# Two tiles per statistics operation, and a VectorE bias in place of a table product, in a graph-network layer on one core

## The chip, the cores and the metric

The kernel runs on one core of a Trainium2 chip. The core has five engines with a queue of instructions each: TensorE (PE in the profile; its weight loads are PEld), VectorE (DVE), ScalarE (ACT), GpSimd (POOL) and SyncE (SP), which here issues DMAs. [...] Matrix products go to PSUM[...]; everything else lies in SBUF. The metric is the time of one execution on the device in microseconds (us), lower is better.

## The reference

128 graphs of 64 nodes with 128 features each. Every pair of nodes gets a message from a three-layer perceptron, the messages are masked by the adjacency matrix and summed, and a second perceptron updates the nodes. Between the layers stand layer normalisations.

```python
def _mlp(x, w0, b0, g0, be0, w1, b1, g1, be1, w2, b2):
    h = relu(x @ w0 + b0)
    h = _layernorm(h, g0, be0)
    h = relu(h @ w1 + b1)
    h = _layernorm(h, g1, be1)
    return h @ w2 + b2

pair_feats = concatenate([f_i, f_j], axis=-1)
messages = _mlp(pair_feats, msg_w0, ..., msg_b2)
messages = messages * coupling_matrix[..., None]
agg = sum(messages, axis=2)
upd_in = concatenate([part_feats, agg], axis=-1)
updated = part_feats + _mlp(upd_in, upd_w0, ..., upd_b2)
```

Only the variance of each normalisation is needed row by row: the mean is taken out by centring the next layer's weights (`w1c`). The scale by 1/std is put off as well. If layer 0's standard deviation is sd, relu((h/sd) @ w1c + b1) is relu(h @ w1c + sd * b1)/sd. So layer 1's bias is a product of a row (b1) and a column (sd of each edge).

## The kernel before, in words

The graph is sparse, so the kernel lists the existing edges only. Two graphs make a pair, a pair has room for 2 x 640 edges, which are ten tiles of 128 edges. Four tiles make a chunk (`CH = 4`), and there are 160 chunks (`NCHK`). Five chunks make a group q of twenty tiles (`QT = 20`, `QC = 5`), of which there are 32 (`NQ`). Four pairs, ten chunks, make a block (`CPB = 10`), which ends in an update of its nodes; a `Unit` is such an update.

A chunk goes through these stages:

- `layer0` (L550): products of PE into the one bank `hps`; ACT takes the relu out of it into `h`, features on the partitions (L559).
- `stats0` (L561): PE transposes the four tiles of `h` into the one bank `hT` (L565), and DVE takes the statistics of each tile by one `bn_stats` (L569). Such an operation gives six numbers per edge: count, mean and squared deviations of the elements at even places, and the same for the odd ones.
- `layer1` (L616): PE adds h @ w1c onto a bank z that already holds sd * b1 (L626), and ACT takes the relu out into `y` (L629). There are two z banks, taken in turn.
- `stats1` (L631): four more `bn_stats`, on `y` in SBUF (L636).
- later the weights (L702, POOL) and the sums over the edges (`reduce`, L717).

After five chunks of `stats0`, `var0_of` (L575) has POOL join the two halves of each statistic into a sum of squares (`square_sum`, L247: five operations of 20 columns), and `root_of` (L578) has ACT take the root, sd. `var1_step` (L638) does the same for layer 1 with the term eps * variance of layer 0. For the last group DVE does it in POOL's place.

The bias sd * b1 comes into a z bank in two ways. In most chunks (those of `seed`, L605, called at L933: digits 0, 1, 2, 5, 6, 7, 9 of n mod 10, from chunk 2 to 151, the first block without 5) ACT writes b1 times the column sd, one tile at a time (L614). In the others, among them the last eight chunks, PE writes it by one product before its own (L623). For this product, `bias_rows` to `bias_part` (L641 to L679) build a table `b1t` of 80 rows at the start, which has b1 in two parts of shorter numbers, and for each group `root_of` splits sd in two parts (L583 on ACT, L584 on POOL), `turn_root` (L587) turns them by PE, and `root_out` (L592) has ACT copy the result to `sdT`.

The order of all work is written out by hand. `at(n, place, fn)` puts a call into step n of a plan, and the loop at the end walks the steps. Within a step the order is: places a, m and s, `layer1` of chunk n - L1 (L1 = 8), place b, `layer0` of chunk n, `stats0` of chunk n - 1, place k, `stats1` of chunk n - L1, places x, x1, x2, e0, e1, e. Each engine takes its share of these calls in just this order. A seed for chunk n stands at place x of step n + 6, so behind `stats1` of chunk n - 2, which used the same z bank. The update units use `square_sum` and `bn_stats` in the same way (`layer_out`, L781; `upd_m0`; `upd_m1`).

Of the kernel before, what the change touches and what calls it, by code (L numbers as in the profile page):

```python
# [9 lines left out]
F32 = mybir.dt.float32  # L10
# [8 lines left out]
EPS = 1e-5  # L19
# [5 lines left out]
def tile_gnn(  # L25
# [221 lines left out]
    def square_sum(stp, st, n, name, eng=nc.gpsimd, m20=None):  # L247

        d = stp.tile([P, n], F32, name=name + "_d")
        s = stp.tile([P, n], F32, name=name + "_s")  # L250
        m2 = stp.tile([P, n], F32, name=name)
        eng.tensor_tensor(d, st[:, :, 1], st[:, :, 4], op=ALU.subtract)  # L252
        eng.tensor_tensor(s, st[:, :, 2], st[:, :, 5], op=ALU.add)
        if eng is nc.vector:
            if m20 is not None:
                eng.scalar_tensor_tensor(s, m20, EPS, s, op0=ALU.mult, op1=ALU.add)
            eng.scalar_tensor_tensor(d, d, C / 4.0, d, op0=ALU.mult, op1=ALU.mult)
        else:
            eng.tensor_tensor(d, d, d, op=ALU.mult)
            eng.tensor_scalar(d, d, C / 4.0, None, op0=ALU.mult)  # L260
        eng.tensor_tensor(m2, d, s, op=ALU.add)
        return m2

# [6 lines left out]
    def var1_of(stp, st, m20, n, name, eng=nc.gpsimd):  # L270

        if eng is nc.vector:
            return square_sum(stp, st, n, name, eng, m20)
        v = stp.tile([P, n], F32, name=name + "_v")
        eng.tensor_scalar(v, m20, EPS, None, op0=ALU.mult)
        m2 = square_sum(stp, st, n, name, eng)
        eng.tensor_tensor(v, v, m2, op=ALU.add)
        return v
# [16 lines left out]
    def rstd1_of(stp, st, m20, n, name):  # L295
        return inverse(stp, root1(stp, var1_of(stp, st, m20, n, name), n, name), n, name)


    def edge_path(es):
# [45 lines left out]
        TP, S, H, ST0, V0, SD, SH, Y, ST1, Q, OH, WT, YS, MK, D, IR, JR, SR, Z = ({} for _ in range(19))  # L345
# [215 lines left out]
        def stats0(n):  # L561
            q, c = divmod(n, QC)
            ps = ps_t.tile([P, CH, P], F32, name="hT")
            for t in range(CH):
                nc.tensor.transpose(ps[:, t, :], H[n][:, t * P:(t + 1) * P], ident)  # L565
            if c == 0:
                ST0[q] = stp.tile([P, QT, 6], F32, name="st0", bufs=2)
            for t in range(CH):
                nc.vector.bn_stats(ST0[q][:, CH * c + t, :], ps[:, t, :])  # L569

        def eng_of(q):

            return nc.vector if q == NQ - 1 else nc.gpsimd

        def var0_of(q):  # L575
            V0[q] = square_sum(stp, ST0.pop(q), QT, "m20", eng_of(q))

        def root_of(q):  # L578

            sd = SR[q] = root0(stp, V0[q], QT, "m20")  # L580
            SH[q] = lp.tile([P, 4, QT], F32R, name="sh", bufs=2)
            sdb = sd.unsqueeze(1).to_broadcast([P, 2, QT])
            nc.scalar.copy(SH[q][:, 0:2, :], sdb)  # L583
            nc.gpsimd.tensor_tensor(SH[q][:, 2:4, :], sdb, SH[q][:, 0:2, :].bitcast(F32),  # L584
                                    op=ALU.subtract)

        def turn_root(q):  # L587
            SD[q] = abank()
            nc.tensor.transpose(SD[q][0:4 * QT, 0:P],
                                SH.pop(q).rearrange("p j t -> p (j t)").bitcast(F32), ident)  # L590

        def root_out(q):  # L592
            t = lp.tile([4 * QT, P], F32R, name="sdT")
            nc.scalar.copy(t, SD[q][0:4 * QT, 0:P])
            SD[q] = t

        SEEDED = set()
# [6 lines left out]

        def seed(n):  # L605

            q, c = divmod(n, QC)
            z_of(n)  # L610
            SEEDED.add(n)
            for t in range(CH):
                k = CH * c + t
                nc.scalar.activation(Z[n][:, t, :], W["b1b"], AF.Copy, scale=SR[q][:, k:k + 1])  # L614

        def layer1(n):  # L616

            q, c = divmod(n, QC)
            ps = z_of(n)
            del Z[n]  # L620
            h = H.pop(n)
            if n not in SEEDED:
                nc.tensor.matmul(ps, lhsT=SD[q], rhs=W["b1t"][:, CH * c:CH * c + CH, :],  # L623
                                 start=True, stop=False, skip_group_check=True)
            for t in range(CH):
                nc.tensor.matmul(ps[:, t, :], lhsT=h[:, t * P:(t + 1) * P], rhs=W["w1c"],  # L626
                                 start=False, stop=True, skip_group_check=True)
            Y[n] = yp.tile([P, CH, C], F32, name="y")
            nc.scalar.activation(Y[n], ps, AF.Relu)  # L629

        def stats1(n):  # L631
            q, c = divmod(n, QC)
            if c == 0:
                ST1[q] = stp.tile([P, QT, 6], F32, name="st1", bufs=2)
            for t in range(CH):
                nc.vector.bn_stats(ST1[q][:, CH * c + t, :], Y[n][:, t, :])  # L636

        def var1_step(q):  # L638
            Q[q] = var1_of(stp, ST1.pop(q), V0.pop(q), QT, "m21", eng_of(q))

        def bias_rows():  # L641

            own = const.tile([P, 4, QT], F32, name="own")
            nc.gpsimd.memset(own, 0.0)
            nc.gpsimd.affine_select(out=own, in_=own, pattern=[[-QT, 4], [-1, QT]],
                                    compare_op=ALU.not_equal, fill=1.0, base=0,
                                    channel_multiplier=1)

            sel = const.tile([P, 2, QT], F32, name="sel")
            nc.gpsimd.tensor_tensor(sel, own[:, 0:2, :], own[:, 2:4, :], op=ALU.add)  # L650
            W["tile_of"] = const.tile([P, QT], F32, name="tile_of")
            nc.gpsimd.tensor_tensor(W["tile_of"], sel[:, 0, :], sel[:, 1, :], op=ALU.add)
            W["sel"] = sel

        def bias_parts():
            W["part"] = const.tile([P, 2], F32, name="part")
            nc.vector.tensor_reduce(W["part"], W.pop("sel"), axis=AX.X, op=ALU.add)

        def bias_table():

            K = 4 * QT
            part, tile_of = W.pop("part"), W["tile_of"]
            hi = const.tile([P, C], F32R, name="b1hi")
            nc.scalar.copy(hi, W["b1b"])
            lo = const.tile([P, C], F32, name="b1lo")
            nc.gpsimd.tensor_tensor(lo, W["b1b"], hi.bitcast(F32), op=ALU.subtract)
            nc.gpsimd.tensor_scalar(lo, lo, part[:, 1:2], None, op0=ALU.mult)
            mix = const.tile([P, C], F32, name="b1mix")
            nc.gpsimd.tensor_scalar(mix, hi.bitcast(F32), part[:, 0:1], None, op0=ALU.mult)
            nc.gpsimd.tensor_tensor(mix, mix, lo, op=ALU.add)  # L670
            W["b1t"] = const.tile([K, QT, C], F32R, name="b1t")
            W["b1mix"], W["tile_of"] = mix[0:K], tile_of[0:K]

        def bias_part(c):
            t = slice(CH * c, CH * c + CH)
            nc.gpsimd.tensor_tensor(W["b1t"][:, t, :],
                                    W["b1mix"].unsqueeze(1).to_broadcast([4 * QT, CH, C]),
                                    W["tile_of"][:, t].unsqueeze(2).to_broadcast([4 * QT, CH, C]),
                                    op=ALU.mult)  # L679
# [101 lines left out]
        def layer_out(u, o, bias):  # L781
            t = wide(o, u)
            add_relu(t, u.l_ps, getattr(u, bias))
            setattr(u, o, t)
            st = updp.tile([P, PB, 6], F32, name=o + "_st", bufs=2)[:, 0:u.n, :]
            for q in range(u.n):
                nc.vector.bn_stats(st[:, q, :], t[:, q, :])
            u.st = st

        def upd_m0(u):  # L790
            u.m2 = square_sum(updp, u.st, u.n, "um0" + u.tag, u.eng)
# [14 lines left out]
        def upd_m1(u):  # L806
            u.v1 = var1_of(updp, u.st, u.m2, u.n, "um1" + u.tag, u.eng)
# [111 lines left out]
        for q in range(NQ):  # L919
# [5 lines left out]
            at(*((n + 1, "x1") if last else (n + 1 if q else QC + 1, "x")), turn_root, q)  # L925
            at(n + 2 if q else QC + 2, "a", root_out, q)
# [6 lines left out]
        for n in range(2, NCHK - L1):  # L933
            if n % CPB in (0, 1, 2, 6, 7, 9) or (n > CPB and n % CPB == 5):
                at(n + L1 - 2, "x", seed, n)


# [25 lines left out]
        bias_rows()  # L963
# [35 lines left out]
        bias_parts()  # L999
# [33 lines left out]
        at(3, "e", bias_table)  # L1033
        for n, k in ((2, 2), (3, 3), (4, 2), (5, 2)):
            at(n, "e", keep_busy, k)
        for c in range(QC):
            at(4 + c, "e", bias_part, c)

# [235 lines left out]
```

## Time and profile before

| | us |
|---|---|
| median of three runs | 549.38 (547.74 to 549.64) |
| the profiled execution | 547.41 |
| its span, first to last instruction | 545.6 |
| PE, DVE, ACT, POOL busy in 200 to 300 us | 100.0, 93.3, 94.3, 67.1 |
| the same in 500 to 520 us | 18.3, 16.3, 11.4, 8.1 |
| the same in 520 to 546 us | 16.4, 14.8, 9.2, 9.1 |
| seeds by ACT, L614 (416 of 128x128) | 154.7 busy, 372 ns each |
| table products, L623 (56 of 80x512) | 26.9 busy, 480 ns each |
| turning of the root, L589 (32) | 9.2 busy, 289 ns each |
| copies for it on ACT, L583 and L594 (32 each) | 7.2 and 8.2 busy |
| small arithmetic of the statistics on POOL, L252 (62 of 128x20) | 15.9 busy, 257 ns each |
| L490, DVE product of 128x512 from PSUM (30) | 20.4 busy, 681 ns each |

Busy time is the time in which an engine works on at least one instruction. An instruction's own duration is longer than the share of time that it takes from its engine, since neighbours overlap: what a queue loses to an instruction is read from the distance between starts in the timeline. The granted clock of PE is 0.995 of full speed over the span.

### The profile page before, as it was taken

What the parts mean: (1) busy time and instruction counts of PE and PEld (TensorE: products, weight loads), DVE (VectorE), ACT (ScalarE), POOL (GpSimd) and SP (SyncE); (2) the same over time, 40 slices, a digit from 0 to 9 for tenths busy, and PEclk for the clock granted to TensorE, in tenths of its full rate; (3) what the DMA queues carried; (4) which work ended last, traced back from release to release, by engine and by line L of the source; (5) the groups of instructions that cost most, each with busy time, mean ns of one, the idle gap of its engine ahead of it and who ended that gap; (6) DMA issues with size and microseconds to landing.
All of it is one profiled execution on the core that took longest, in us unless ns stands there. A gap on an engine that the chain in (4) does not pass through costs nothing. (4 is left out here: it accounts for less than half of the span.)

```text
span 545.6 us, 16370 instructions
## 1 busy us (share of the span) xinstructions
PE 526.1 (96%) x5599; PEld 483.6 (89%) x5599; DVE 479.5 (88%) x1941; ACT 479.6 (88%) x1153; POOL 328.8 (60%) x934
## 2 busy tenths in 40 slices
PE   8999899999999999999999999999999999998984
PEld 7787789999999999999999999999999999988873
DVE  6778789898989899898989989898999989897765
ACT  6788989898999999999999989999999999996534
POOL 3445466665657676665667666566766666556342
PEclk9999999999999999999999999999999999999998
DMA  4484655545684545547555564558456544651401
GB/s 101 103 163 112 145 98 139 119 117 123 120 158 109 143 117 129 127 101 167 119 134 102 140 128 112 145 122 142 113 140 128 123 112 113 142 96 25 46 22 44
DMA packets 90772, 63.26 MB, mean 116 GB/s; under 512 B 57398, under 2 KB 74812, under 8 KB 90684
## 3 DMA queue, kind: packets, MB, share of 16 engines
q1 hardware_dynamic: 90396, 62.03, 52.8%
q8 instruction: 46, 0.75, 0.6%
q14 instruction: 42, 0.34, 0.2%
q10 hardware_dynamic: 288, 0.13, 0.1%
HBM read 6.82 MB, written 4.19 MB: 20 GB/s over the span
## 5 line engine op out<-in xcount | busy, mean ns | idle before, releaser
L626 PE MATMUL z<-w1c,h 128*128 128x128 f32 x1280 | 172.0, 277 | 0.0
L626 PEld LDWEIGHTS z<-w1c,h 128*128 128x128 f32 x1280 | 160.7, 192 | 7.7 <-issue 2.8
L614 ACT ACTIVATE z<-b1b,m_sd 128x128 f32<-128x128 f32 x416 | 154.7, 372 | 10.1
L569 DVE BATCH_NORM_STATS2 st<-hT 128x6 f32<-128x128 f32 x640 | 139.7, 279 | 21.4 <-PE hT L565 21.3
L636 DVE BATCH_NORM_STATS2 st<-y 128x6 f32<-128x128 f32 x640 | 137.5, 276 | 1.9 <-ACT y L629 1.4
L629 ACT ACTIVATE y<-z 128x512 f32<-128x512 f32 x160 | 94.9, 593 | 20.3 <-PE z L626 19.6
L559 ACT ACTIVATE h<-hps,b0c 128x512 f32<-128x512 f32 x160 | 109.8, 686 | 1.1 <-PE hps L556 1.0
L565 PE MATMUL hT<-ident,h 128*128 128x128 f32 x640 | 97.7, 275 | 2.1 <-DVE st L569 1.6
L556 PE MATMUL hps<-s,abl 128*128 128x512 f32 (+3 forms) x256 | 91.8, 370 | 0.9 <-ACT h L559 0.4
L565 PEld LDWEIGHTS hT<-ident,h 128*128 128x128 f32 x640 | 74.5, 141 | 15.8 <-DVE st L569 7.1
L556 PE MATMUL hps<-s,abh 128*128 128x512 f32 (+3 forms) x256 | 77.9, 323 | 0.0
L702 POOL TENSOR_TENSOR w<-oh,m_q 128x192 f32<-128x192 f16 x126 | 64.7, 526 | 4.5 <-PE ys L717 3.3
L252 POOL TENSOR_TENSOR m_d<-st 128x20 f32<-128x20 f32 x62 | 15.9, 257 | 76.0 <-DVE st L569 62.2
L538 DVE TENSOR_TENSOR j<-mk,cmpt 128x320 fp32r<-128x320 f32 x124 | 58.6, 473 | 1.0 <-PE mk L530 1.0
L514 POOL CAST i<-tp 128x640 fp32r<-128x640 f16 x58 | 41.6, 718 | 27.9 <-issue 15.1
L499 ACT ACTIVATE d<-slot,mid 128x640 f16<-128x640 f16 x64 | 53.2, 831 | 0.2 <-DVE mid L423 0.2
L556 PEld LDWEIGHTS hps<-s,abl 128*128 128x128 f32 x256 | 48.9, 191 | 1.8 <-ACT h L559 0.9
L556 PEld LDWEIGHTS hps<-s,abh 128*128 128x128 f32 x256 | 48.9, 191 | 0.0
L717 PE MATMUL ys<-y,w 128*32 128x128 f32 x1488 | 47.0, 275 | 0.0
L717 PEld LDWEIGHTS ys<-y,w 128*32 128x32 f32 x1488 | 38.7, 110 | 4.1 <-issue 3.6
L490 DVE TENSOR_TENSOR abl<-mu,abh 128x512 fp32r<-128x512 f32 (+1 forms) x32 | 21.3, 664 | 19.6 <-ACT abh L484 19.6
L530 PE MATMUL mk<-tp,posall 128*128 128x320 f16 x126 | 37.7, 299 | 0.4 <-DVE tp L505 0.4
(243 smaller groups left out, 991.1 us busy)
## 6 DMA issues: line engine op xcount, KB each, us to landing
s<-i SPq DMA_DIRECT2D x124, 160.0 KB, 2.7
s<-j SPq DMA_DIRECT2D x124, 160.0 KB, 2.7
xn<-in_x_dram SPq DMA_DIRECT2D x15, 256.0 KB, 3.9
out_dram<-uo SPq DMA_DIRECT2D x15, 256.0 KB, 2.4
an<-in_adj_dram SPq DMA_DIRECT2D x16, 128.0 KB, 2.8
oh<-tp SPq DMA_TRANSPOSE x64, 3.5
xn<-in_x_dram SPq DMA_DIRECT2D x2, 128.0 KB
out_dram<-uo SPq DMA_DIRECT2D x2, 128.0 KB, 2.6
```

The source lines that it names most:

```text
L499: nc.scalar.activation(D[p], slot, AF.Abs, bias=blocks[b]["mid"][:, q:q + 1], scale=-1.0)
L538: nc.vector.tensor_tensor(JR[p][:, c], MK.pop((p, k))[:, 0:HC], cmpt[:, c], op=ALU.is_equal)
L556: nc.tensor.matmul(ps[:, c:c + w], lhsT=ab[:, g % 4, :], rhs=s, start=(k == 0), stop=(k == 1))
L559: nc.scalar.activation(H[n], ps, AF.Relu, bias=b0c)
L565: nc.tensor.transpose(ps[:, t, :], H[n][:, t * P:(t + 1) * P], ident)
L569: nc.vector.bn_stats(ST0[q][:, CH * c + t, :], ps[:, t, :])
L614: nc.scalar.activation(Z[n][:, t, :], W["b1b"], AF.Copy, scale=SR[q][:, k:k + 1])
L626: nc.tensor.matmul(ps[:, t, :], lhsT=h[:, t * P:(t + 1) * P], rhs=W["w1c"], start=False, stop=True, skip_group_check=True)
L629: nc.scalar.activation(Y[n], ps, AF.Relu)
L636: nc.vector.bn_stats(ST1[q][:, CH * c + t, :], Y[n][:, t, :])
L702: (nc.vector if p == NP - 2 else nc.gpsimd).tensor_tensor(WT[p][:, g], oh, qs, op=ALU.mult)
L717: nc.tensor.matmul(YS[b][g * N + m * HN:g * N + (m + 1) * HN, k, :], lhsT=w[:, g, m, u, :], rhs=y, start=(u == 0), stop=(u == TH - 1), til ...
```

## The change

Statistics: two tiles are taken by one `bn_stats`. Its stream takes an element of the first tile, then one of the second, and so on, so that the elements at even places are the first tile and those at odd places the second. The two sums of squared deviations that come out are those of the two tiles, and nothing has to be joined: `var0_of` becomes a view, and layer 1's variance is the view plus the term of layer 0, two operations on POOL in place of seven. This holds for the edge tiles (hT in PSUM, y in SBUF) and for the update.

Bias: the table, its building and the turning of the root are gone. Chunks with the digits 3, 4 and 8 (in the first block 1 and 5 too) and the odd ones of the last eight get their bias from DVE, by one product of 128x512 into the z bank; ACT seeds those that it did, and chunk 0 and the even ones of the last eight. Two products `prime` the z banks at the start.

```diff
+    def two_stats(st, src):
+
+        nc.vector.bn_stats(st, src.rearrange("p t c -> p c t"))
+
+    def squares_of(st):
+        return st.rearrange("p t (h k) -> p (t h) k", h=2)[:, :, 2]
...
             if c == 0:
-                ST0[q] = stp.tile([P, QT, 6], F32, name="st0", bufs=2)
-            for t in range(CH):
-                nc.vector.bn_stats(ST0[q][:, CH * c + t, :], ps[:, t, :])
+                ST0[q] = stp.tile([P, QT // 2, 6], F32, name="st0", bufs=6)
+            for t in range(0, CH, 2):
+                two_stats(ST0[q][:, (CH * c + t) // 2, :], ps[:, t:t + 2, :])
...
         def var0_of(q):
-            V0[q] = square_sum(stp, ST0.pop(q), QT, "m20", eng_of(q))
+            V0[q] = squares_of(ST0.pop(q))
 
         def root_of(q):
 
-            sd = SR[q] = root0(stp, V0[q], QT, "m20")
-            SH[q] = lp.tile([P, 4, QT], F32R, name="sh", bufs=2)
...
+            SR[q] = root0(stp, V0[q], QT, "m20")
...
+        def prime(n):
+            nc.tensor.matmul(z_of(n), lhsT=slot[:, 0:P], rhs=cmpt[:, 0:CH * C], start=True,
+                             stop=True, skip_group_check=True)
+
         def seed(n):
...
             q, c = divmod(n, QC)
-            z_of(n)
-            SEEDED.add(n)
+            z = z_of(n)
+            k = CH * c
+            if by_vector(n):
+                nc.vector.tensor_tensor(
+                    z, bc(W["b1b"], CH),
+                    SR[q][:, k:k + CH].unsqueeze(2).to_broadcast([P, CH, C]), op=ALU.mult)
+                return
             for t in range(CH):
-                k = CH * c + t
-                nc.scalar.activation(Z[n][:, t, :], W["b1b"], AF.Copy, scale=SR[q][:, k:k + 1])
+                nc.scalar.activation(z[:, t, :], W["b1b"], AF.Copy,
+                                     scale=SR[q][:, k + t:k + t + 1])
...
         def layer1(n):
 
-            q, c = divmod(n, QC)
-            ps = z_of(n)
-            del Z[n]
+            ps = Z.pop(n)
             h = H.pop(n)
-            if n not in SEEDED:
-                nc.tensor.matmul(ps, lhsT=SD[q], rhs=W["b1t"][:, CH * c:CH * c + CH, :],
-                                 start=True, stop=False, skip_group_check=True)
             for t in range(CH):
...
-        for n in range(2, NCHK - L1):
-            if n % CPB in (0, 1, 2, 6, 7, 9) or (n > CPB and n % CPB == 5):
-                at(n + L1 - 2, "x", seed, n)
...
+        def by_vector(n):
+            if n >= NCHK - L1:
+                return n % 2 == 1
+            return n % CPB in (3, 4, 8) or (n < CPB and n % CPB in (1, 5))
+
+        for n in range(2):
+            at(L1 - 1 - n, "s", prime, n)
+            at(L1 - 1, "x", seed, n)
+        for n in range(2, NCHK):
+            at(n + L1 - 2, "x", seed, n)
```

More of the change, by code (lines that the diff above doesn't have):

```diff
@@ L245, in add_relu, with square_sum @@
         nc.vector._custom_dve(TENSOR_ADD_SAT, out=o, in0=ps, in1=sb, s0=BIG, s1=0.0)
-    def square_sum(stp, st, n, name, eng=nc.gpsimd, m20=None):
+    def square_sum(stp, st, n, name):
         d = stp.tile([P, n], F32, name=name + "_d")
@@ L251, in square_sum @@
         m2 = stp.tile([P, n], F32, name=name)
[L252 to L261, printed above, removed]
-        return m2
+        nc.gpsimd.tensor_tensor(d, st[:, :, 1], st[:, :, 4], op=ALU.subtract)
+        nc.gpsimd.tensor_tensor(s, st[:, :, 2], st[:, :, 5], op=ALU.add)
+        nc.gpsimd.tensor_tensor(d, d, d, op=ALU.mult)
+        nc.gpsimd.tensor_scalar(d, d, C / 4.0, None, op0=ALU.mult)
+        nc.gpsimd.tensor_tensor(m2, d, s, op=ALU.add)
+        return m2
+    def two_stats(st, src):
+        nc.vector.bn_stats(st, src.rearrange("p t c -> p c t"))
+    def squares_of(st):
+        return st.rearrange("p t (h k) -> p (t h) k", h=2)[:, :, 2]
     def root0(stp, m2, n, name):
@@ L268, in root0, with var1_of @@
         return sd
-    def var1_of(stp, st, m20, n, name, eng=nc.gpsimd):
+    def var1_of(stp, m21, m20, n, name, eng):
+        v = stp.tile([P, n], F32, name=name + "_v")
         if eng is nc.vector:
-            return square_sum(stp, st, n, name, eng, m20)
-        v = stp.tile([P, n], F32, name=name + "_v")
+            eng.scalar_tensor_tensor(v, m20, EPS, m21, op0=ALU.mult, op1=ALU.add)
+            return v
         eng.tensor_scalar(v, m20, EPS, None, op0=ALU.mult)
-        m2 = square_sum(stp, st, n, name, eng)
-        eng.tensor_tensor(v, v, m2, op=ALU.add)
+        eng.tensor_tensor(v, v, m21, op=ALU.add)
         return v
@@ L295, in rstd1_of @@
     def rstd1_of(stp, st, m20, n, name):
-        return inverse(stp, root1(stp, var1_of(stp, st, m20, n, name), n, name), n, name)
+        v = var1_of(stp, square_sum(stp, st, n, name), m20, n, name, nc.gpsimd)
+        return inverse(stp, root1(stp, v, n, name), n, name)
     def edge_path(es):
@@ L344, in edge_path @@
         blocks = {b: {} for b in range(NB)}
-        TP, S, H, ST0, V0, SD, SH, Y, ST1, Q, OH, WT, YS, MK, D, IR, JR, SR, Z = ({} for _ in range(19))
+        TP, S, H, ST0, V0, Y, ST1, Q, OH, WT, YS, MK, D, IR, JR, SR, Z = ({} for _ in range(17))
         def load_adj(b):
@@ L575, in var0_of @@
         def var0_of(q):
-            V0[q] = square_sum(stp, ST0.pop(q), QT, "m20", eng_of(q))
+            V0[q] = squares_of(ST0.pop(q))
         def root_of(q):
-            sd = SR[q] = root0(stp, V0[q], QT, "m20")
-            SH[q] = lp.tile([P, 4, QT], F32R, name="sh", bufs=2)
[L582 to L597, printed above, removed]
+            SR[q] = root0(stp, V0[q], QT, "m20")
         def z_of(n):
@@ L633, in stats1 @@
             if c == 0:
-                ST1[q] = stp.tile([P, QT, 6], F32, name="st1", bufs=2)
-            for t in range(CH):
-                nc.vector.bn_stats(ST1[q][:, CH * c + t, :], Y[n][:, t, :])
+                ST1[q] = stp.tile([P, QT // 2, 6], F32, name="st1", bufs=2)
+            for t in range(0, CH, 2):
+                two_stats(ST1[q][:, (CH * c + t) // 2, :], Y[n][:, t:t + 2, :])
         def var1_step(q):
-            Q[q] = var1_of(stp, ST1.pop(q), V0.pop(q), QT, "m21", eng_of(q))
@@ L641, in bias_rows @@
[L641 to L679, printed above, removed]
+            Q[q] = var1_of(stp, squares_of(ST1.pop(q)), V0.pop(q), QT, "m21", eng_of(q))
         def root1_of(q):
@@ L784, in layer_out @@
             setattr(u, o, t)
-            st = updp.tile([P, PB, 6], F32, name=o + "_st", bufs=2)[:, 0:u.n, :]
-            for q in range(u.n):
-                nc.vector.bn_stats(st[:, q, :], t[:, q, :])
+            st = updp.tile([P, PB // 2, 6], F32, name=o + "_st", bufs=2)[:, 0:u.n // 2, :]
+            for q in range(0, u.n, 2):
+                two_stats(st[:, q // 2, :], t[:, q:q + 2, :])
             u.st = st
         def upd_m0(u):
-            u.m2 = square_sum(updp, u.st, u.n, "um0" + u.tag, u.eng)
+            u.m2 = squares_of(u.st)
         def upd_root0(u):
@@ L806, in upd_m1 @@
         def upd_m1(u):
-            u.v1 = var1_of(updp, u.st, u.m2, u.n, "um1" + u.tag, u.eng)
+            u.v1 = var1_of(updp, squares_of(u.st), u.m2, u.n, "um1" + u.tag, u.eng)
         def upd_root1(u):
@@ L924, in edge_path @@
             at(*((n, "e0") if last else (n + 1, "b")), root_of, q)
-            at(*((n + 1, "x1") if last else (n + 1 if q else QC + 1, "x")), turn_root, q)
-            at(n + 2 if q else QC + 2, "a", root_out, q)
             at(end - last, "e1", var1_step, q)
@@ L962, in edge_path @@
         place_rest()
-        bias_rows()
         rows(0, 0, 0, 2)
@@ L998, in edge_path @@
         distance(2)
-        bias_parts()
         marks_here(1)
@@ L1032, in edge_path @@
             at(n + 1, "m", lambda k=k, empty=empty: empty(W.pop(("ps", k))))
-        at(3, "e", bias_table)
         for n, k in ((2, 2), (3, 3), (4, 2), (5, 2)):
             at(n, "e", keep_busy, k)
-        for c in range(QC):
-            at(4 + c, "e", bias_part, c)
         fl = const.tile([P, 3], F32, name="fl")
```

## The prediction

> **What bounds the kernel now.** I read the page's first part, then the stages, the waits, the groups and the timeline of ten chunks in the middle.
>
> ```profile
> PE 526.1 (96%) x5599; PEld 483.6 (89%) x5599; DVE 479.5 (88%) x1941; ACT 479.6 (88%) x1153; POOL 328.8 (60%) x934
> ...
> 140.13:453.40 313.27, 313.27 (x3440) 292.69 (x3434) 291.20 (x1182) 294.85 (x711) 206.30 (x582) 1.00 0.59 127
> ```
> The second line is a stretch of ten periods of ten chunks (the L751 groups recur every 31.33 us). PE never rests in it, ACT is busy 29.5 us of a period and DVE 29.1. The three engines are near each other, so the question is which one is last when one gets shorter.
>
> ```profile
> DVE st L569 <- PE hT L565: 21.3, 42, 2.2
> ...
> ACT y L629 <- PE z L626: 19.6, 29, 2.6
> ...
> PEld hT L565 <- DVE st L569: 7.1, 19, 0.6
> ...
> PEld z L626 <- ACT z L614: 2.4, 14, 0.2
> ```
> In the waits DVE and ACT wait for PE for 20 us each; PE waits for them for some 10. So PE sets the pace, with DVE and ACT only 6% behind it.
>
> ```profile
> 302.44 0.60 PE L763 MATMUL ma<-ident,uy 128*128 128x128 f32 x4
> 302.80 0.48 PE L623 MATMUL z<-b1t,sdT 80*128 80x512 f32 x1
> 303.11 1.05 PE L626 MATMUL z<-w1c,h 128*128 128x128 f32 x8
> ...
> 302.81 0.82 DVE L569 BATCH_NORM_STATS2 st<-hT 128x6 f32<-128x128 f32 x4
> 303.55 0.47 DVE L538 TENSOR_TENSOR j<-mk,cmpt 128x320 fp32r<-128x320 f32 x1
> 303.94 0.86 DVE L636 BATCH_NORM_STATS2 st<-y 128x6 f32<-128x128 f32 x4
> ...
> L569 DVE BATCH_NORM_STATS2 st<-hT 128x6 f32<-128x128 f32 x640 | 139.7, 279 | 21.4 <-PE hT L565 21.3
> L636 DVE BATCH_NORM_STATS2 st<-y 128x6 f32<-128x128 f32 x640 | 137.5, 276 | 1.9 <-ACT y L629 1.4
> ```
> A table product (L623) holds PE from 302.80 to 303.11, 0.31 us, though its row says 0.48: instructions overlap, so what counts is the distance between starts. Four statistics take 0.86 us with 0.276 for the last one, so they start (0.86 - 0.276)/3 = 0.195 us apart.
>
> [...]
>
> **The change part by part**, per period of ten chunks unless said.
>
> *Off PE.* Three table products at 0.315 us (the mean over the 30 in the stretch, from each start to the next one's), 0.945. Two transposes of the root (L589): in the PE timeline one holds PE for 0.14 us (306.99 to 307.13), one for 0.03, so 0.17 together. Sum 1.11 us of 31.33. Over the whole kernel 56 x 0.315 + 32 x 0.085 = 20.4 us; the stretch where PE is full, 60 to 500 us, has 14 periods, 15.6 us. Two prime products (under 1 us in all) fall in the start, where PE has gaps.
>
> *Off ACT.* Two casts to `sh` (224 ns) and two to `sdT` (256 ns); by their distances in the timeline 0.13 and 0.16, so 0.57 us. ACT seeds 436 tiles in place of 416, all 20 more in the first chunk and in the last eight. So ACT has 29.5 - 0.57 = 28.9 us per period, against a PE period of 30.2: it still fits, at 96%.
>
> *Off POOL.* Nearly all small statistics arithmetic (L252 to L261 and the hi/lo split), and in the start the building of the table (five L676 of 1.1 us). POOL was 60% busy; nothing ends there.
>
> *DVE, statistics.* 40 pairs of edge tiles and 4 of the update. Now a pair costs 2 x 0.195 = 0.39 us. [...] I take full rate[...]. [...]
>
> *DVE, seeds.* A 128x512 product written to PSUM is in no row. Nearest is L490, 128x512 from PSUM, 681 ns long and 0.60 from its start to the next one's. I take 0.60: three per period, +1.8 us; 51 in all, 31 us. [...] upper end 0.9[...]: the two DVE weight products at 523.28 have the same shape and took 359 and 664 ns, the second one beside POOL's. DVE then has 29.1 - 2.6 + 1.8 = 28.3 us: it fits in 30.2.
>
> *The new wait.* A table product waited for nothing; layer 1 now waits for DVE's seed. It stands behind the statistics of the chunk two before. At 303.11: DVE ends those statistics at 302.44, the seed would end near 303.0, and PE, without the table, wants it at 302.80. The shorter statistics give 0.2 back. At 319.71 it is the same: statistics end 319.12, seed 319.75, PE wants it at 319.39. The third seed has a us to spare. So 0.1 to 0.2 us of stall twice, 0.3 per period, 4 us over 14. Behind a seed in DVE's queue stand the reciprocal `m_q` and the next chunk's statistics; the transposes already wait for these (the 7.1 us above), and they end earlier at full rate: 2 us back.
>
> *Start and end.* The first layer 1 stands at 32.4 us behind the derivation's products, not the table alone. In the end the last eight layer 1 start from 508.0 to 518.2. With seeds each waits for y of two chunks before: product 0.81, [...]relu 0.6, then 4 x 0.31 on ACT, or two statistics and 0.6 on DVE: 3.0 us per two chunks, against 2.9 now. Nothing is gained there; the root's way (cast, subtract, transpose, cast) was not what PE waited for. 0 to -1 us, taken as 0.
>
> Sum: -15.6 + 4 - 2 = -13.6 us. On the profiled execution's 547.41 this is 533.8. The median is 2.0 us above it (549.38), so 536 for a median.
>
> **Rivals.**
>
> 1. *The alternating stream is slow* (ends slower). Place: every two-tile statistic. [...] It decides from a pair spacing of 0.40 us (29.1 + 1.8 + 44 x 0.01 = 31.3, the present period)[...]. [...]
> 2. *Three full engines.* The rate is full, but ACT at 96% and the seed waits hold the period at 31.0 or more: 545 to 552. For it: each of the three is within 7% of the period, and the hps, hT and z banks have no spare copies. Against it: ACT loses work too, and its waits for PE (19.6) shrink first.
> 3. [...] At 0.9 us a seed DVE is at 29.2 of 30.2 and the two tight seeds are late by 0.4 each: 0.6 more per period, -13.6 + 8 = -5, 544. This counts as faster.
>
> **How the numbers follow.** About 0.5% (2.7 us) is what a measurement of this kernel tells from no change. The forecast: 0.47, own range 528 to 541. Rival 3: 0.10, 540 to 546. Rival 2: 0.08, of which 0.06 is no change and 0.02 slower. Rival 1: 0.35, half of it with one memory slow (556 to 582) and half with both (600 to 630). So faster 0.57, same 0.06, slower 0.37. The range leaves out both-slow and the edges: 527 to 582.
>
> **What would show it.** The row of the two-tile statistics decides[...]. Seeds by DVE near 0.69 us long; PE full with periods of 30.2 to 30.6 us; no L623; waits of PE on DVE's z below 6 us in all. I am wrong if DVE is the engine without gaps, or if the rows of hT and y differ.

## The result and the profile after

The changed kernel takes 544.21 us (median of five runs, 543.9 to 545.64), the kernel before 549.23 in the runs beside it. The ratio of the means is 0.9924, 95% interval 0.9901 to 0.9947. It is faster by 0.8%, where 2.4% was forecast. The direction was right; two thirds of the gain are missing. Runs of one kernel fall in two groups some 2 us apart (before: 547.74 and 547.76, and 549.23 to 549.64), so small differences are read from the period in the middle of the kernel, 140 to 450 us, where the granted clock is 1.00 in every profile.

The page of the changed kernel, first its busy times, then the groups of the two-tile statistics:

```profile
PE 520.0 (96%) x5513; PEld 471.6 (87%) x5513; DVE 472.3 (87%) x1271; ACT 475.0 (88%) x1108; POOL 207.4 (38%) x419
...
L261 DVE BATCH_NORM_STATS2 st<-hT 128x6 f32<-128x256 f32 x320 | 118.8, 412 | 20.5 <-PE hT L568 18.3
L261 DVE BATCH_NORM_STATS2 st<-y 128x6 f32<-128x256 f32 x320 | 120.7, 418 | 4.2 <-ACT y L617 4.2
```

The statistics are not what is missing. 412 and 418 ns for 256 elements are the 279 and 276 ns of one tile plus 128 elements at 1.04 and 1.11 ns. Between one tile and the 512 elements of L490 in the kernel before (279 and 681 ns) an element costs 1.05 ns. By that measure the alternating stream runs at full rate, from PSUM as from SBUF. But PE is still busy for 96% of the span, only 6 us less than before, and DVE's total fell by 7 us only. The loss is in the periods. The same ten periods as before (31.17 us each now, by the distance of the bias rows; 31.33 before) lie in this stretch; the columns are PE, PEld, DVE, ACT and POOL, the granted clock, and the DMA share with its GB/s:

```profile
138.90:450.60 311.70, 311.17 (x3391) 285.17 (x3384) 289.16 (x772) 289.01 (x671) 134.45 (x261) 1.00 0.57 128
```

PE has lost three products and two transposes per period, yet the period is only 0.16 us shorter. Who waited in this stretch:

```profile
PEld hT L568 <- PE z L614: 6.5, 20, 0.4
...
PEld z L614 <- DVE z L601: 4.2, 20, 0.2
```

Twice per period layer 1 (L614) waits some 0.2 us for a seed of DVE (L601), 4.2 us in ten periods; a kernel with table products has no such wait. A second thing stands out: a group that the change does not touch, the update's four bias rows (`bias0`, L751 before, L699 now), takes longer. DVE's and POOL's timelines, before and then after:

```profile
296.77 1.18 DVE L751 SCALAR_TENSOR_TENSOR m<-c2u,deg,ub0b 128x128 f32<-128x128 f32 x4
...
296.77 0.25 POOL L252 TENSOR_TENSOR m_d<-st 128x20 f32<-128x20 f32 x1
296.98 0.28 POOL L253 TENSOR_TENSOR m_s<-st 128x20 f32<-128x20 f32 x1
297.22 0.28 POOL L259 TENSOR_TENSOR m_d<-m_d 128x20 f32<-128x20 f32 x1
297.60 0.27 POOL L260 TENSOR_SCALAR m_d<-m_d 128x20 f32<-128x20 f32 x1
297.94 0.23 POOL L261 TENSOR_TENSOR m<-m_d,m_s 128x20 f32<-128x20 f32 x1
298.25 0.23 POOL L277 TENSOR_TENSOR m_v<-m_v,m 128x20 f32<-128x20 f32 x1
298.43 1.53 POOL L413 TENSOR_TENSOR posall<-pos,an 64x256 f16<-64x256 f32 x2
```
```profile
294.72 1.90 DVE L699 SCALAR_TENSOR_TENSOR m<-c2u,deg,ub0b 128x128 f32<-128x128 f32 x4
296.54 0.75 DVE L261 BATCH_NORM_STATS2 st<-hT 128x6 f32<-128x256 f32 x2
...
294.17 0.27 POOL L279 TENSOR_TENSOR m_v<-m_v,st 128x20 f32<-128x20 f32 x1 [1.30 <-DVE st L261]
294.40 1.54 POOL L416 TENSOR_TENSOR posall<-pos,an 64x256 f16<-64x256 f32 x2
```

Before, POOL had its six small operations to do while DVE computed the bias rows, and came to its long position products (`posall`) when DVE was through. All but the last of these are what the change removes. Now POOL has only L279 left, which waits for a statistic of DVE, and `posall` starts 0.3 us before DVE's bias rows. The four rows take 1.90 us in place of 1.18.

### The profile page after: what moved, and what is told of

It reads as the page before. It is cut to its first block, busy times and chain, and to the rows that moved or that the text cites. A ratio compares the mean times of both kernels' runs of the same rounds, so it can differ in the third digit from the quotient of the medians.

```text
span 542.4 us, 15157 instructions
## 1 busy us (share of the span) xinstructions
PE 520.0 (96%) x5513; PEld 471.6 (87%) x5513; DVE 472.3 (87%) x1271; ACT 475.0 (88%) x1108; POOL 207.4 (38%) x419
## 5 line engine op out<-in xcount | busy, mean ns | idle before, releaser
L614 PE MATMUL z<-w1c,h 128*128 128x128 f32 x1280 | 175.8, 280 | 5.2 <-DVE z L601 2.5
L614 PEld LDWEIGHTS z<-w1c,h 128*128 128x128 f32 x1280 | 155.6, 191 | 18.8 <-DVE z L601 8.6
L606 ACT ACTIVATE z<-b1b,m_sd 128x128 f32<-128x128 f32 x436 | 162.1, 372 | 10.7
L261 DVE BATCH_NORM_STATS2 st<-hT 128x6 f32<-128x256 f32 x320 | 118.8, 412 | 20.5 <-PE hT L568 18.3
L261 DVE BATCH_NORM_STATS2 st<-y 128x6 f32<-128x256 f32 x320 | 120.7, 418 | 4.2 <-ACT y L617 4.2
L650 POOL TENSOR_TENSOR w<-oh,m_q 128x192 f32<-128x192 f16 x126 | 61.5, 510 | 59.9 <-PE ma L711 25.9
L279 POOL TENSOR_TENSOR m_v<-m_v,st 128x20 f32<-128x20 f32 x31 | 7.7, 250 | 78.3 <-DVE st L261 74.7
```

The source lines that it names most:

```text
L261: nc.vector.bn_stats(st, src.rearrange("p t c -> p c t"))
L606: nc.scalar.activation(z[:, t, :], W["b1b"], AF.Copy, scale=SR[q][:, k + t:k + t + 1])
L650: (nc.vector if p == NP - 2 else nc.gpsimd).tensor_tensor(WT[p][:, g], oh, qs, op=ALU.mult)
```

## The experiments

Eleven kernels ran. The ratio is to the kernel before on the same chip, and the period is the mean distance of the bias rows of successive blocks in the full stretch. Compare ratios and periods, not times: in the batches of e1 to e11 the kernel before took 547.6 to 547.9 us. The recorded expectations weigh theories against each other. The collision theory says that the longer bias rows cost the time; the queue-order theory, that a seed stands too late in DVE's queue; the no-room theory, that the sum of each engine's work sets the period. The loop theory came after the first four runs and is explained below.

| kernel | us | ratio (95% interval) | period, us |
|---|---|---|---|
| before | 549.23 | 1 | 31.33 |
| after | 544.21 | 0.9924 (0.9901 to 0.9947) | 31.17 |
| e1, statistics alone | 541.7 | 0.9884 (0.9864 to 0.9904) | 31.19 |
| e2, bias by DVE alone | 561.47 | 1.023 (1.0208 to 1.0252) | 31.91 |
| e3, posall one step later | 544.01 | 0.9923 (0.9907 to 0.9939) | 31.17 |
| e4, seed ahead of statistics | 541.28 | 0.9874 (0.9851 to 0.9896) | 31.03 |
| e5, bias rows in DVE's gap | 540.13 | 0.9861 (0.9833 to 0.9890) | 30.77 |
| e6, no seeds by DVE | 531.11 | 0.9681 (0.9655 to 0.9707) | 30.29 |
| e7, posall earlier | 540.9 | 0.9859 (0.9836 to 0.9882) | 30.75 |
| e8, e5 and e4 | 539.29 | 0.9841 (0.9818 to 0.9865) | 30.89 |
| e9, e1 and e5's move | 541.73 | 0.9884 (0.9864 to 0.9904) | 31.21 |
| e10, e7 and an earlier tp | 535.65 | 0.9776 (0.9757 to 0.9795) | 30.51 |
| e11, e5 and an earlier tp | 537.01 | 0.9783 (0.9762 to 0.9804) | 30.50 |

### The two halves of the change, each alone

e1 is the kernel before with `two_stats` and `squares_of`, the table products kept:

```diff
-            for t in range(CH):
-                nc.vector.bn_stats(ST0[q][:, CH * c + t, :], ps[:, t, :])
+            for t in range(0, CH, 2):
+                two_stats(ST0[q][:, (CH * c + t) // 2, :], ps[:, t:t + 2, :])
...
```

> The kernel before with two-tile statistics alone; the table products and the turning of the root stay. Collision theory (POOL's position product now starts with DVE's bias rows[...]): the four bias rows (scalar_tensor_tensor m<-c2u,deg,ub0b) take about 1.9 us as in the changed kernel, yet no product of PE waits for a seed of DVE, so PE keeps its 31.3 us period: 0.995 to 1.000 of before. If instead the statistics themselves carry the gain: 0.99 of before, as the whole change. A two-tile statistic shows 412 to 418 ns in both.

e2 is the changed kernel with one statistic per tile again, and `square_sum` on POOL:

```diff
-            for t in range(0, CH, 2):
-                two_stats(ST0[q][:, (CH * c + t) // 2, :], ps[:, t:t + 2, :])
+            for t in range(CH):
+                nc.vector.bn_stats(ST0[q][:, CH * c + t, :], ps[:, t, :])
...
```

> The changed kernel with one-tile statistics and POOL's joining of halves put back; seeds by DVE stay. DVE then has 29.1 + 1.8 = 30.9 us of work in a period. If DVE's room is what the change needs: DVE without gaps, period 31.5 to 32.5, 1.00 to 1.03 of before. If DVE's room does not matter (only the order of its queue does): about as the changed kernel, 0.99 of before.

The statistics alone bring 1.2%, more than the collision theory allowed (0 to 0.5%) and near what the second theory said; the bias alone costs 2.3%. Together they bring 0.8%, and the intervals of e1 and of the whole overlap only at their edges: beside two-tile statistics, taking three products per period off PE was worth nothing, or less than nothing.

In the full stretch it was worth nothing: 31.19 us in e1, 31.17 with the whole change. What the whole loses to e1 lies at the start and at the end. The first layer 1 starts at 34.5 us, in e1 at 32.2 (32.4 before), and the last eight start over 12.7 us, in e1 over 10.2 (10.2 before). In both places layer 1 now waits for seeds, of ACT too; at the start this wait is 0.6 of the 2.3 us, and where the rest comes from was not followed up:

```profile
34.48 1.16 PE L614 MATMUL z<-w1c,h 128*128 128x128 f32 x8 [0.60 <-ACT z L606]
...
514.34 1.16 PE L614 MATMUL z<-w1c,h 128*128 128x128 f32 x8 [0.32 <-ACT z L606]
...
516.70 1.13 PE L614 MATMUL z<-w1c,h 128*128 128x128 f32 x8 [1.20 <-DVE z L601]
```

e2 fits the theory that the change needs DVE's room: its period, 31.91, is in the range given for it. It does not prove it. DVE is busy 296.34 us of 310 there, so it is not without gaps, and e2 also brings back POOL's joining of the halves, for which ACT now waits 0.9 us per period. e2 does not separate the two.

```profile
ACT m_sd L267 <- POOL m L261: 8.0, 9, 0.9
```

In e1 the bias rows take 1.89 us too (with them moved, in e9, DVE is busy for 269.66 of 310 us in place of 274.57), so the collision comes with the statistics, not with the seeds. It does no harm there, since no product of PE waits for a seed of DVE (e9, below, takes it away and gains nothing).

### The collision, a first try and a second

e3 and e7 move one call, by one step, in opposite directions:

```diff
-                at(*((r + 2, "a") if b == 1 else (o - 7, "e")), place_out, b)
+                at(*((r + 2, "a") if b == 1 else (o - 6, "e")), place_out, b)
```
```diff
-                at(*((r + 2, "a") if b == 1 else (o - 7, "e")), place_out, b)
+                at(*((r + 2, "a") if b == 1 else (o - 8, "e")), place_out, b)
```

> The changed kernel with POOL's position products (posall<-pos,an) one step later; DVE's order is untouched. Collision theory: the four bias rows fall from 1.9 to 1.1 us, DVE comes 0.8 us earlier to the seed of digit 8 and to the bank hT, waits of PE there (0.39 us per period) vanish: 5 us less than the changed kernel, 538 to 540. Queue-order theory and no-room theory: the rows get shorter but the time stays within 1.5 us of the changed kernel's 544.2.

> The changed kernel with POOL's position products ahead of the small variance operations in POOL's queue, so that they run before DVE comes to the bias rows; DVE's order is untouched. Collision theory: the four bias rows take 1.1 to 1.2 us in place of 1.9, the two waits behind them (0.39 us per period) go: period 30.75 to 30.85, 538 to 540. If the collision does not count: rows shorter, period 31.1 or more, within 1.5 us of 544.2.

e3 is a miss of mine: between the two steps POOL has no other instruction, so its queue is the same as in the changed kernel, and so are the rows (1.89 us) and the time. It decides nothing. e7 puts the products ahead of four small operations, two of which wait for DVE. In its timeline of DVE and POOL the products are over before the rows begin:

```profile
292.36 1.13 DVE L699 SCALAR_TENSOR_TENSOR m<-c2u,deg,ub0b 128x128 f32<-128x128 f32 x4
...
288.84 1.52 POOL L416 TENSOR_TENSOR posall<-pos,an 64x256 f16<-64x256 f32 x2
...
291.82 0.27 POOL L279 TENSOR_TENSOR m_v<-m_v,st 128x20 f32<-128x20 f32 x1 [0.62 <-DVE st L261]
```

The rows take 1.13 us, the period falls from 31.17 to 30.75, the ratio to 0.9859. The period is what the collision theory gave; the median, 540.9, is just above its range. The order of DVE, ACT and PE is the same instruction for instruction, so this part of the loss, 0.42 us per period, is shown to be the collision. Single rows show it too: in the changed kernel the 26 of 64 that ran beside `posall` took 554 to 886 ns, the 38 others 331 to 360, and in e7 none took over 364. In the collision shown above POOL's two products end at 295.13 and 295.95 us, and the two long rows (562 and 886 ns) each some 0.15 us later; the two rows behind them take 340 ns again. What holds them up there is not shown.

### Why 0.7 us of DVE cost PE 0.4: a loop

After the first four runs I replaced "which engine is full" by a loop, read from the changed kernel's timeline of DVE:

```profile
313.93 0.69 DVE L493 TENSOR_TENSOR abl<-mu,abh 128x512 fp32r<-128x512 f32 x1 [1.52 <-ACT abh L487]
314.54 1.11 DVE L508 TENSOR_SCALAR tp<-d,deg 128x640 f16<-128x640 f16 x1
315.57 0.75 DVE L261 BATCH_NORM_STATS2 st<-hT 128x6 f32<-128x256 f32 x2
316.24 0.75 DVE L261 BATCH_NORM_STATS2 st<-y 128x6 f32<-128x256 f32 x2
316.91 0.68 DVE L601 TENSOR_TENSOR z<-b1b,m_sd 128x512 f32<-128x512 f32 x1
317.50 0.27 DVE L290 RECIPROCAL m_q<-m_sq 128x20 f32<-128x20 f32 x1
```

Once per period DVE stands idle for 1.52 us, in front of the subtraction `abl<-mu,abh`, which waits for ACT's copy `abh` (313.31 to 313.90), which waits for PE's node rows (`mu`). From 313.93 on DVE has no wait until it has written the seed of digit 8, 18.5 us later. PE's layer 1 starts behind that seed and from then on PE runs without a gap to the end of the next node rows, 12.0 us; ACT's copy takes 0.6, and DVE's next subtraction follows. These are the joints, from the timelines of DVE, PE and ACT:

```profile
331.72 0.68 DVE L601 TENSOR_TENSOR z<-b1b,m_sd 128x512 f32<-128x512 f32 x1
332.46 1.16 PE L614 MATMUL z<-w1c,h 128*128 128x128 f32 x8
...
344.47 0.59 ACT L487 CAST abh<-mu 128x512 fp32r<-128x512 f32 x1 [0.56 <-PE mu L475]
345.09 0.69 DVE L493 TENSOR_TENSOR abl<-mu,abh 128x512 fp32r<-128x512 f32 x1 [1.52 <-ACT abh L487]
```

Together 31.1 us, the period. What is taken from DVE in the first part, or from PE in the second, should shorten the loop until another wait becomes the tightest; what is taken from DVE where it idles, or from PE where it waits for a seed, should not. e7 shows the limit: the rows lost 0.77 us, the period 0.42, and one of the two waits for a seed is still in its list (2.1 us in ten periods).

e4 puts DVE's seeds ahead of the statistics of y:

```diff
-            at(n + L1 - 2, "x", seed, n)
+            at(n + L1 - 2, "k" if by_vector(n) else "x", seed, n)
```

> The changed kernel with DVE's seeds ahead of the two statistics of y in DVE's queue, 0.67 us earlier. Queue-order theory: the waits of PE on DVE's z (0.47 us per period, 14 periods) vanish, 537 to 539. Collision theory: only the seeds of digits 3 and 4 gain, 541 to 542. No-room theory (ACT, DVE and PE all full): the wait moves elsewhere, within 1 us of 544.2.

The wait for seeds is gone from the list of waits, but only 0.14 us per period is won. PE now waits at the bank `hT`, for statistics that stand behind the same seed:

```profile
PE hT L568 <- DVE st L261: 4.3, 10, 0.4
```

So the queue-order theory named a place but not the cause. Its 541.28 is where the collision theory had put it, by a way that that theory did not name.

e5 leaves POOL alone and moves the bias rows into DVE's idle stretch:

```diff
-                at(n + m0_at, "e" if b == NB - 1 else "m", bias0, u)
+                at(n + (-4 if b < NB - 3 else m0_at), "e" if b == NB - 1 else "a" if b < NB - 3 else "m", bias0, u)
```

> The changed kernel with the update's four bias rows (m<-c2u,deg,ub0b) moved in DVE's queue to just ahead of the subtraction abl<-mu,abh, where DVE stands idle 1.5 us per period. Loop theory: the period is a loop, DVE's unbroken work from that subtraction to the seed of digit 8, then PE's unbroken work from that chunk's layer 1 to the node rows, then ACT's copy abh back to the subtraction. The move takes 1.9 us out of DVE's part: period 30.4 to 30.8 in place of 31.17, 534 to 539. No-room theory (the sum of each engine's work sets the period): 31.1, within 1.5 us of 544.2.

The period, 30.77 us, is within what the loop theory said and far from the no-room theory; the time, 540.13, is above the loop theory's 534 to 539, though nearer to it than to 544.2. The same move in e1 (e9), where PE does not wait for seeds:

> Two-tile statistics alone (table products kept) with the same move of the bias rows. If PE's own work holds that kernel's period (31.19 us): no gain, within 1 us of its 541.7, and then the room on PE is worth 3 to 6 us once DVE's part is shortened (compare the same move on the changed kernel). If DVE's part holds it too: 30.8, 536 to 538.

It gains nothing, as the first theory there had it: DVE's part does not hold e1's period. And the changed kernel without any seed by DVE (e6), whose 51 chunks go without this bias; the first of their products has `start=True`:

```diff
             if by_vector(n):
-                nc.vector.tensor_tensor(
-                    z, bc(W["b1b"], CH),
-                    SR[q][:, k:k + CH].unsqueeze(2).to_broadcast([P, CH, C]), op=ALU.mult)
                 return
...
```

> The changed kernel without DVE's seeds: the 51 chunks have no bias[...]. It shows what DVE's seeds cost in all. Loop theory: DVE's part of the loop is 0.6 us shorter and PE does not wait at the two seeds: period 30.5 to 30.7, 535 to 538. No-room theory with ACT as the full engine: ACT's work is the same, period 31.0 or more, 542 to 544.

The period is 30.29 us, shorter than I had put it, and so is the time. In the same stretch, 140 to 450 us, PE has no gap in e6 and none in e1. It has none in the kernel before either, so this alone says little (first line e6, second e1, third before):

```profile
140.00:450.00 310.00, 310.00 (x3443) 290.79 (x3442) 281.52 (x761) 293.84 (x687) 133.23 (x267) 1.00 0.59 131
```
```profile
140.00:450.00 310.00, 310.00 (x3404) 291.10 (x3406) 274.57 (x737) 293.01 (x706) 134.04 (x280) 1.00 0.59 128
```
```profile
140.00:450.00 310.00, 310.00 (x3388) 289.67 (x3377) 287.97 (x1167) 291.68 (x704) 203.44 (x571) 1.00 0.58 127
```

The lists of waits tell them apart: in this stretch PE's weight loads wait for DVE and ACT in the kernel before (3.2 and 1.7 us), and PE waits for neither in e1 and e6. So I take both periods as PE's own work, with and without the table products and the turning of the root: 31.19 - 30.29 = 0.90 us is what the change takes off PE. DVE's seeds give 31.17 - 30.29 = 0.88 of it back. ACT was not the limit: it is busier in e6 (293.84 of 310) than in the changed kernel.

### Versions that beat both

In the first timeline of the loop, at 314.54, `tp<-d,deg` (L508) takes 1.11 us, although it takes 377 ns in the median. POOL's timeline of the changed kernel shows what runs beside it:

```profile
314.42 1.04 POOL L748 TENSOR_TENSOR usdb<-bu1b,um_sd 128x512 f32<-128x512 f32 x1 [3.73 <-DMA s<-j]
```

The kernel before had this collision too (1.10 to 1.11 us in its full stretch), but no seed behind it. e10 is e7 with this operation put into DVE's idle stretch, e11 is e5 with the same:

```diff
-                    at(max(n - 6, p - 2), "m", make_tp, p)
+                    at(max(n - 6, p - 2), "a" if p % PB == 2 and p > PB else "m", make_tp, p)
```

> The kernel with POOL's position products earlier, and DVE's comparison tp<-d,deg of every fourth pair put ahead of the subtraction abl<-mu,abh, into DVE's idle stretch. There it no longer meets POOL's product usdb (1.11 us beside it, 0.35 alone). Loop theory: 1.1 us less in DVE's part, the seed of digit 3 in time: period 30.3 to 30.5 in place of 30.75, 3 to 6 us less than 540.9, that is 535 to 538. If only the seed of digit 8 counted: 30.7, within 1.5 us of 540.9.

> The changed kernel with both the bias rows and that comparison in DVE's idle stretch ahead of the subtraction (1.05 + 0.35 us in a stretch of 1.5). Loop theory: as the kernel before it or better, period 30.3 to 30.4, PE's own work (30.29 without any seed of DVE): 534 to 537. If the idle stretch is overfilled, the subtraction itself is late, node rows wait: 30.6 or more, 539.

In e10's timeline of DVE the operation takes 0.37 us in the idle stretch, and now DVE waits for PE ahead of the statistics in front of the first seed:

```profile
307.14 0.37 DVE L508 TENSOR_SCALAR tp<-d,deg 128x640 f16<-128x640 f16 x1
308.76 0.69 DVE L493 TENSOR_TENSOR abl<-mu,abh 128x512 fp32r<-128x512 f32 x1 [1.25 <-ACT abh L487]
310.12 0.76 DVE L261 BATCH_NORM_STATS2 st<-hT 128x6 f32<-128x256 f32 x2 [0.68 <-PE hT L568]
310.80 0.76 DVE L261 BATCH_NORM_STATS2 st<-y 128x6 f32<-128x256 f32 x2
311.47 0.69 DVE L601 TENSOR_TENSOR z<-b1b,m_sd 128x512 f32<-128x512 f32 x1
```

PE's waits for DVE are no longer in the list, and the period is 30.51, some 0.2 us above PE's own work. The time is 535.65 us, by the ratios 2.2% below the kernel before and 1.5% below the change as it was made. e10 takes the operation out of the loop and out of its collision at once; how much of the 0.24 us per period belongs to which is not shown. e11 does as well within its interval. e8 is e5 with e4's earlier seed:

> The bias rows in the idle stretch, and DVE's seeds ahead of the statistics of y. Loop theory: both seeds in time, but the statistics of hT behind them come 0.6 us later and PE waits there: 30.5 to 30.7, 536 to 540. If the wait for the seed were all that is lost: 30.3, 533 to 536.

e8's time fits the first theory, but its period, 30.89, is outside the 30.5 to 30.7 given and longer than that of e5 without the earlier seed. PE waits 4.3 us in ten periods at `hT`, as in e4. The earlier seed only moves the wait.

## Why the forecast was too high, step by step

*Statistics.* Right: full rate in both memories, a pair 0.33 us from the next by their starts in the timeline. Against the 0.39 of two one-tile statistics that is 0.06 us less, 2.6 us per period over 44 pairs, the forecast's figure, which was the author's estimate. The slower rate behind rival 1's times is shown by no trace. Rival 1 is out.

*Seeds.* Right in price: 680 ns in the median, 0.59 from start to start, and none much longer than that (784 at most).

*Off PE.* Mis-sized: 1.11 us per period was put down, 0.90 measured (e1 against e6). I had taken the distance between a product's start and the next one's as its cost; part of it is what the transposes in front hand on. Their next start comes 0.08 us sooner before a table product than before a layer 1 (behind L763 in the kernel before, 0.03 us against 0.11).

*Off POOL.* This is the step that failed: "POOL was 60% busy; nothing ends there". It looked only at what waits for POOL. But an engine with less to do also does the rest sooner, and POOL's next long operation then fell together with DVE's bias rows and made them longer, 1.90 us in place of 1.18. Their row was known (350 ns each) and was left out of the sum. The forecast's sum amounts to a period of 30.36 us (13.6 us over 14 periods); 31.17 was measured, 0.81 more. The collision is 0.42 of it (e7). In the profiled runs e7's span is 4.9 us shorter than the changed kernel's; by the ratios it is 3.6 us.

*DVE's room.* "28.3 us: it fits in 30.2" was a sum, and the sum was nearly right (28.9 by its busy time). It missed that DVE's work between the node rows and a seed lies in a loop with PE's. Moving one operation of DVE out of that part won another 0.24 us (e10 against e7).

*The new wait.* 0.3 us per period was put down, 0.42 is in the list of waits (4.2 us in ten periods). The place was right, both tight seeds. What came with it was missed: with PE's and DVE's work in one loop, the transposes to `hT` wait behind the seeds as well, where the forecast had credited 2 us for shorter statistics.

*Rival 3* gave 544 us by seeds of 0.9 us beside POOL, and 544.2 was measured. That is chance in part: 50 of the 51 seeds took 671 to 692 ns. That an operation of DVE takes longer beside POOL's was right at another instruction, the bias rows, and the prediction's search stopped at the instructions that the change adds.

*Rival 2* came near as well: a period of 31.0 or more, held by seed waits. Its reason, three full engines, is refuted by e6 and e10: the same ACT work fits in 30.3 and 30.5 us.

*Start and end.* 0 was put down for the bias there. Against e1 it cost 1.4 us up to the first product of layer 1 for chunk 20, and 2.5 us over the last eight chunks: these come at 3.6 us per two, where 3.0 was forecast (0.81, 0.6 and 4 x 0.31 add to 2.65; the rest was the author's estimate of the hand-over from PE to ACT, which in the kernel before takes 0.28 us, from PE's next product at 508.81 to the relu at 509.09). In the comparison with the kernel before the shorter statistics hide this: its span and the changed kernel's differ by 2.2 us between the first products of layer 1 for chunks 20 and 140, and by 1.0 us outside, both in favour of the change.

What stays open: the 0.2 us per period between e10 and e6, what e10's gain is made of, and how much of e2's loss is DVE's room.

## What to carry to other kernels

When a change takes work off an engine that nobody waits for, ask what that engine will now start earlier, and beside what: two engines can collide at instructions that the change does not touch, as POOL's `posall` and DVE's bias rows did here (1.90 us in place of 1.18). When several engines are near full, the sum of each engine's work says little; follow one period around the waits, see which stretches of which engine lie in the loop, and put work that can move where its engine idles. And try the parts of a change alone: here the enabling half was worth more than the whole, until work of DVE was moved out of the loop (e10, e11).

## What was not expected of the hardware

A statistic over a stream that alternates between two tiles 512 bytes apart runs at full rate, 412 to 418 ns for 256 elements in the mean, from PSUM and from SBUF (1.04 and 1.11 ns for each element that the second tile adds). The collision with GpSimd spares the statistics, which read one input: of 640 over edge tiles in the changed kernel none took over 437 ns, though 379 ran beside some instruction of POOL; in the kernel before, 89 one-tile statistics ran beside `posall` and took 266 to 291 ns. The comparison `tp<-d,deg` also reads one tensor, of fp16, beside one number per partition. It took 0.35 to 0.39 us where it met no product of POOL, and 1.10 to 1.11 beside POOL's product `usdb` (12 of 13 times in the changed kernel, 0.86 in the last). What sets it apart from the statistics was not tested.
